# Pairwise bilinear products on one core: three equal store slots in the output ring, two-tile loads of x from GpSimd, and the last load of W without its zeros

## The chip, the cores and the metric

The kernel runs on one core of a Trainium2 chip. The metric is the device time of one execution in microseconds (us). The kernel before was run nine times: the median is 1323.14 us, the lowest 1320.26, the highest 1325.19. A separate profiled execution of it took 1322.69 us.

## The reference, cut to what matters

The input x has 4096 rows, each with 32 fields of 64 numbers (float32). For every pair of fields i < j, 496 in all, there is a 64 x 64 matrix W. The output for a pair is the product of field i with W, multiplied element by element with field j:

```python
i_idx, j_idx = np.triu_indices(32, k=1)
vi = inputs[:, i_idx, :]
vj = inputs[:, j_idx, :]
vdotw = jnp.einsum('bpd,pde->bpe', vi, W)
inter = vdotw * vj
return inter.reshape(B, -1)          # 4096 x (496 * 64)
```

The output is 520 MB, x 33.6 MB, W 8.1 MB. So the kernel writes far more than it reads.

## The kernel before, in words

**Tiles.** The 4096 rows are cut into 32 tiles of 128 rows; a tile puts one row on each partition. The loop over `t` goes through the tiles, and inside it a loop goes through 16 pairs of fields `p`: fields 2p and 2p+1 are first factors together. Field i has 31 - i partners, so its output row segment is (31 - i) units of 64 numbers wide; a tile's output is 496 such units. A unit over 128 partitions is 32,768 bytes.

**Matrix work.** `transpose_x` transposes half a tile on PE (8 blocks of two fields) into PSUM, and ACT copies it to `xT`. Field 2p then lies in the upper 64 partitions and field 2p+1 in the lower 64. For each chunk of up to 512 columns PE multiplies both fields with their columns of W into two banks of the PSUM ring `pring` (8 banks), and VectorE (DVE) multiplies the two banks with the columns of x into the output ring `ring` in SBUF. The transposes of a tile's second half come before pair 3 of the tile; those of the first half come before pair 9 of the tile before it (`SECOND_HALF_AT`, `FIRST_HALF_AT`).

**W.** W is kept in SBUF for the whole kernel: even fields in the upper 64 partitions, odd fields in the lower 64, shifted by one unit, with zeros where the odd rows are shorter. SP loads it in five pieces (`LOADS`), the last for pairs 7 to 15.

**Stores.** `STORES` cuts the 16 pairs of a tile into four groups of 118, 102, 123 and 153 units. When a group is computed, SP issues one DMA of it from the ring to the output, with rows of 26 to 39 KB per partition. The ring has 440 units (`RING = 28160` columns). A group is never split at the ring's end: if it doesn't fit, it begins at the start again,

```python
if at + store_w[s] > RING:
    at = 0
```

and the units behind it stay unused in that round. VectorE may write a part of the ring again only when the store that reads it has landed.

**Loads of x.** Three slots in SBUF hold tiles. Load 0 brings tile 0, loads 1 to 15 bring two tiles each, load 16 brings tile 31. Load k is issued at the start of tile 2k - 2. Tiles in `LIGHT_TILES` (13 even ones) are loaded by GpSimd alone, one tile at a time in rows of 8 KB; the odd tile of the same load is then brought by ACT. The other loads are one ACT DMA each: two with rows of 16 KB for two tiles, two with one tile.

**The DMA engines.** A core has 16 DMA engines. The GpSimd loads are arranged so that engine 4 (`LIGHT`) carries none of them: `load_beside` sends 120 rows, 8 to each of 15 engines that begin with number 5, and the last 8 rows as 4 rows each to two other engines, which `PAIRS_FROM` names in turn. Which engine a GpSimd DMA begins with is kept in `cursor`; `from_engine` moves it on with a tiny DMA, a nudge. So one such load is four DMAs on GpSimd's queue: nudge, 8 rows, nudge, 120 rows. They are kept in program order. The pieces of x in memory are padded so that the access patterns keep this shape; the pads are not read.

Of the kernel before, what the change touches and what calls it, by code (L numbers as in the profile page):

```python
# [9 lines left out]
F32 = mybir.dt.float32  # L10
ALU = mybir.AluOpType

P = 128
BANK = 512
BANKS = 8

STORES = [[0, 1], [2, 3], [4, 5, 6], [7, 8, 9, 10, 11, 12, 13, 14, 15]]

LOADS = [[0], [1], [2, 3], [4, 5, 6], [7, 8, 9, 10, 11, 12, 13, 14, 15]]


FIRST_HALF_AT, SECOND_HALF_AT = 9, 3
RING = 28160

DMA_ENGINES = 16
LIGHT = 4
LIGHT_TILES = [4, 6, 8, 10, 12, 14, 18, 20, 22, 24, 26, 28, 30]
PAIRS_FROM = [6, 8, 10, 12, 14, 0, 1]
HEAD = P // DMA_ENGINES
REST = HEAD // 2  # L30
PAD = 16


def x_slots(NT):


    loads = [[(0, 0)]]
    for t in range(1, NT, 2):
        if t + 1 == NT:
            loads.append([(t, 1)])  # L40
        elif loads[-1][-1] == (t - 1, 2):
            loads.append([(t + 1, 0), (t, 1)])
        else:
            loads.append([(t, 1), (t + 1, 2)])
    return loads


@with_exitstack
def pair_bilinear_kernel(
    ctx: ExitStack,  # L50
    tc: tile.TileContext,
    x: bass.AP,
    w: bass.AP,
    out: bass.AP,
    F: int,
    D: int,
):

    nc = tc.nc
    NT = out.shape[1] * 2 // (F * (F - 1) * D)
    NPR = F // 2

    width = [(F - 1 - i) * D for i in range(F)]
    off = [sum(width[:i]) for i in range(F)]
    cols = sum(width)


    woff = [i % 2 * D + sum(width[i % 2 : i : 2]) for i in range(F)]
    store_w = [sum(width[2 * p] + width[2 * p + 1] for p in g) for g in STORES]

    const = ctx.enter_context(tc.tile_pool(name="const", bufs=1))
    psum = ctx.enter_context(tc.tile_pool(name="ps", bufs=1, space=bass.MemoryType.PSUM))

    ident = const.tile([P, P], F32, tag="ident", name="ident")
    make_identity(nc, ident)

    def runs(tl, a, b, n):  # L100

        ap = tl[:, a : a + n]
        return bass.AP(ap.tensor, ap.offset, [list(ap.ap[0]), [b - a, 2], list(ap.ap[1])])

    xbuf = const.tile([P, 3 * F * D], F32, tag="x", name="x")
    x_loads = x_slots(NT)
    pads = (DMA_ENGINES + 1) * PAD
    tile_sizes = [P * F * D + (pads if t in LIGHT_TILES else 0) for t in range(NT)]
    x_sizes = [sum(tile_sizes[t] for t, s in load) for load in x_loads]
    slot = {t: xbuf[:, ts(s, F * D)] for load in x_loads for t, s in load}  # L110

    nudges = [const.tile([DMA_ENGINES, 16], F32, tag=f"nudge{i}", name=f"nudge{i}") for i in range(2)]
    cursor = 0

    def from_pool(out, in_):

        tc.keep_in_program_order(nc.gpsimd.dma_start(out=out, in_=in_))  # L117

    def from_engine(e):

        nonlocal cursor
        k = (e - cursor) % DMA_ENGINES
        if k:
            nudge = nudges[e == LIGHT + 1]
            from_pool(
                nudge[:k].rearrange("p (h c) -> p h c", h=2)[:, :, :4],
                x[: k * 8].rearrange("(p h c) -> p h c", p=k, h=2),
            )
        cursor = e

    def load_beside(at, xt, lap):

        nonlocal cursor
        most = DMA_ENGINES - 1
        for e, k, rows, p in (
            (PAIRS_FROM[lap % len(PAIRS_FROM)], 2, REST, most * HEAD),
            (LIGHT + 1, most, HEAD, 0),
        ):
            from_engine(e)
            n = rows * F * D  # L140
            blocks = x[at : at + k * (n + PAD)].rearrange("(k c) -> k c", k=k)
            from_pool(xt[p : p + k * rows], blocks[:, :n])
            at += k * (n + PAD)
            cursor = (e + k) % DMA_ENGINES

    def load_x(load):

        at = sum(x_sizes[: x_loads.index(load)])
        parts = [[(t, s)] for t, s in load] if any(t in LIGHT_TILES for t, s in load) else [load]
        for part in parts:  # L150
            t, s = part[0]
            n = len(part) * F * D
            if t in LIGHT_TILES:
                load_beside(at, slot[t], LIGHT_TILES.index(t))
            else:
                nc.scalar.dma_start(
                    out=xbuf[:, s * F * D : s * F * D + n],
                    in_=x[at : at + P * n].rearrange("(p c) -> p c", p=P),
                )
            at += sum(tile_sizes[t] for t, s in part)  # L160

    pring = psum.tile([P, BANKS * BANK], F32, tag="pring", name="pring")
    bank = 0

    def take_banks(n):

        nonlocal bank
        if bank + n > BANKS:
            bank = 0
        got = pring[:, bank * BANK : (bank + n) * BANK]  # L170
        bank = (bank + n) % BANKS
        return got

    xT = const.tile([P, NPR * P], F32, tag="xT", name="xT")

    def transpose_x(xt, g):

        n = 2 * BANK // P
        pt = take_banks(2)
        for c in range(n):  # L180
            nc.tensor.transpose(pt[:, ts(c, P)], xt[:, ts(n * g + c, P)], ident)  # L181
        nc.scalar.copy(xT[:, ts(g, 2 * BANK)], pt)  # L182

    ring = const.tile([P, RING], F32, tag="ring", name="ring")
    at = 0

    load_x(x_loads[0])
    w_sb = const.tile([P, sum(width[0::2])], F32, tag="w", name="w")
    done = 0
    for g in LOADS:  # L190

        upto = woff[2 * g[-1]] + width[2 * g[-1]]
        nc.sync.dma_start(out=w_sb[:, done:upto], in_=w[:, done:upto])
        done = upto

    transpose_x(slot[0], 0)
    for t in range(NT):
        xt = slot[t]
        for load in x_loads:
            if min(load)[0] == t + 1:  # L200
                load_x(load)
        for s, group in enumerate(STORES):
            if at + store_w[s] > RING:
                at = 0
            osb = ring[:, at : at + store_w[s]]
            at += store_w[s]
            o0 = off[2 * group[0]]
            for p in group:
                if p == SECOND_HALF_AT:
                    transpose_x(xt, 1)  # L210
                if p == FIRST_HALF_AT and t + 1 < NT:
                    transpose_x(slot[t + 1], 0)
                first = (width[2 * p] - 1) % BANK + 1
                for c1 in range(first, width[2 * p] + 1, BANK):
                    n = first if c1 == first else BANK
                    c0 = c1 - n
                    odd = width[2 * p + 1] and c1 > D
                    pm = take_banks(2)
                    for h in range(1 + bool(odd)):
                        a = woff[2 * p + h] + c0 - h * D  # L220
                        nc.tensor.matmul(  # L221
                            pm[:, h * BANK : h * BANK + n],
                            xT[h * D : (h + 1) * D, ts(p, P)],
                            w_sb[h * D : (h + 1) * D, a : a + n],
                            start=True,
                            stop=True,
                        )
                    xj = xt[:, (2 * p + 1) * D + c0 : (2 * p + 1) * D + c1]
                    o = [off[2 * p + h] - o0 + c0 - h * D for h in range(2)]
                    if odd and (c0 or c1 < width[2 * p]):  # L230
                        nc.vector.tensor_tensor(  # L231
                            runs(osb, o[0], o[1], n),
                            runs(pm, 0, BANK, n),
                            bass.AP(xj.tensor, xj.offset, [xj.ap[0], [0, 2], xj.ap[1]]),
                            ALU.mult,
                        )
                    else:
                        for h in range(1 + bool(odd)):
                            nc.vector.tensor_tensor(  # L239
                                osb[:, o[h] + h * D : o[h] + n],  # L240
                                pm[:, h * (BANK + D) : h * BANK + n],
                                xj[:, h * D :],
                                ALU.mult,
                            )
            nc.sync.dma_start(
                out=out[:, t * cols + o0 : t * cols + o0 + store_w[s]], in_=osb
            )


# [46 lines left out]
```

## Time and profile before

| What | Value |
|---|---|
| Median of the runs | 1323.14 us (1320.26 to 1325.19) |
| The profiled execution | 1322.69 us, its span 1320.6 us |
| PE (TensorE) busy | 1163.6 us, 88% |
| DVE (VectorE) busy | 1183.4 us, 90%, 1376 instructions |
| ACT (ScalarE), POOL (GpSimd) busy | 66.1 us and 30.2 us |
| DMA | 562.9 MB in 25,404 packets, 426 GB/s over the span |
| Read, written in memory | 41.95 MB, 520.09 MB |

The span is the time from the first to the last instruction on the core; the profiled execution's own time has 2.1 us more around it. The page gives busy time by engine, then 40 equal slices of the span (33 us each) with the busy share in tenths and the rate of the DMA engines in GB/s. Of a DMA queue it tells the packets, the bytes and the share of the 16 engines' span: q1 is SP's queue, q10 ACT's, q0 GpSimd's. Of a group of DMAs it tells how many there are, the size of each and the median time from issue to landing. A line of waits names who waited, for whom, the total in us, how many times, and the longest.

### The profile page before, as it was taken

The numbers are of one execution on the slowest core, as the hardware profiler recorded it, in microseconds if no ns is written. First come the engines' busy times: TensorE is split into PE (matmuls) and PEld (weight loads), VectorE is DVE, ScalarE is ACT, GpSimd is POOL, SyncE is SP. The second block draws the span as 40 slices with busy tenths as digits, with TensorE's granted clock in tenths as the row PEclk, the third lists the DMA queues.
The fourth block names the chain that finished last, engine by engine and source line by source line (L and its number), as shares of the span: only waits on it lengthen the run. The fifth ranks groups of instructions, "written<-read, shape, count | busy, mean of one in ns | idle before, by whom it ended". The sixth has DMA issues, their size and how long they took to land.

```text
span 1320.6 us, 13176 instructions
## 1 busy us (share of the span) xinstructions
PE 1163.6 (88%) x5376; PEld 539.1 (41%) x5376; DVE 1183.4 (90%) x1376; ACT 66.1 (5%) x65; POOL 30.2 (2%) x58
## 2 busy tenths in 40 slices
PE   7998989889898898998899889888988989899993
PEld 3444344343444434444334444334444444343441
DVE  5998999989899898998899899889988989899994
ACT  1000000000000000000000000000000000000000
POOL 0000000000000000000000000000000000000000
PEclk9998999999899998998999989999998999999997
DMA  9999999999999999999999999999999999999998
GB/s 393 431 431 433 427 432 430 426 433 426 427 429 436 419 427 431 431 429 430 426 427 427 430 430 419 433 425 429 429 428 428 416 432 420 437 429 432 427 430 375
DMA packets 25404, 562.90 MB, mean 426 GB/s; under 512 B 4480, under 2 KB 4480, under 8 KB 4736
## 3 DMA queue, kind: packets, MB, share of 16 engines
q1 hardware_dynamic: 19152, 528.49, 93.5%
q10 hardware_dynamic: 2448, 19.92, 3.6%
q0 software_dynamic: 3744, 13.65, 2.5%
q8 instruction: 42, 0.69, 0.2%
q14 instruction: 18, 0.15, 0.0%
HBM read 41.95 MB, written 520.09 MB: 426 GB/s over the span
## 4 chain that ended last, share of the span: by engine, by line
DMA 49%; DVE 34%; PE 8%; issue 8%; DVEq 0%; ACT 0%
DMA out_dram<-ring 49%; DVE ring L231 29%; PE pring L221 7%; DVE ring L239 5%; DMA x<-in_x_dram 1%; DVEq L231 0%; PE pring L181 0%; ACT xT L182 0%; DVEq L292 0%; DVEq L239 0%
## 5 line engine op out<-in xcount | busy, mean ns | idle before, releaser
L221 PE MATMUL pring<-w,xT 64*128 64x512 f32 (+4 forms) x4864 | 1100.4, 562 | 128.5 <-DVE ring L231 108.9
L231 DVE TENSOR_TENSOR ring<-pring,x 128x1024 f32<-128x1024 f32 (+3 forms) x1056 | 1104.8, 1108 | 107.4 <-DMA out_dram<-ring 73.8
L221 PEld LDWEIGHTS pring<-w,xT 64*128 64x128 f32 x4864 | 483.5, 190 | 703.3 <-DVE ring L231 516.4
L182 ACT COPY xT<-pring 128x1024 f32<-128x1024 f32 x64 | 64.8, 1012 | 1209.3 <-PE pring L181 1209.3
L239 DVE TENSOR_TENSOR ring<-pring,x 128x64 f32<-128x64 f32 (+3 forms) x320 | 97.7, 356 | 11.8 <-DMA out_dram<-ring 11.5
L181 PEld LDWEIGHTS pring<-ident,x 128*128 128x128 f32 x512 | 55.7, 142 | 58.1 <-DVE ring L231 49.7
L181 PE MATMUL pring<-ident,x 128*128 128x128 f32 x512 | 70.9, 282 | 8.5 <-DMA x<-in_x_dram 8.4
L117 POOL DMA_DIRECT2D x<-in_x_dram x26 | 15.2, 585 | 1077.9 <-DVE ring L239 1077.6
L117 POOL DMA_DIRECT2D nudge<-in_x_dram x26 | 14.6, 560 | 0.3 <-issue 0.3
L182 ACT ACT_TABLE_LOAD x1 | 1.3, 1283 | 1.7 <-PEq L288 1.7
masks.py:199 POOL TENSOR_SCALAR_AFFINE_SELECT ident<-ident 128x128 f32<-128x128 f32 x1 | 0.3, 288 | 0.1
masks.py:197 POOL MEMSET ident<- 128x128 f32 x1 | 0.2, 204 | 0.3 <-POOLq L288 0.3
L288 POOL MEMSET const-float32-0.0<- 128x1 f32 x1 | 0.1, 98 | 0.2 <-issue 0.2
L288 POOL MEMSET const-bfloat16-1.0<- 128x1 bf16 x1 | 0.1, 101 | 0.0
L288 POOL MEMSET const-uint8-127<- 128x1 uint8 x1 | 0.1, 101 | 0.0
L288 POOL MEMSET const-float32-1.0<- 128x1 f32 x1 | 0.1, 98 | 0.0
## 6 DMA issues: line engine op xcount, KB each, us to landing
out_dram<-ring SPq DMA_DIRECT2D x32, 4896.0 KB, 18.1
out_dram<-ring SPq DMA_DIRECT2D x32, 3936.0 KB, 17.8
out_dram<-ring SPq DMA_DIRECT2D x32, 3776.0 KB, 19.7
out_dram<-ring SPq DMA_DIRECT2D x32, 3264.0 KB, 19.7
x<-in_x_dram ACTq DMA_DIRECT2D x15, 1024.0 KB, 18.6
x<-in_x_dram POOLq DMA_DIRECT2D x13, 960.0 KB, 26.2
x<-in_x_dram ACTq DMA_DIRECT2D x2, 2048.0 KB, 18.2
w<-in_w_dram SPq DMA_DIRECT2D x1, 2592.0 KB, 28.0
```

The lines of the kernel that those rows point to most:

```text
L117: tc.keep_in_program_order(nc.gpsimd.dma_start(out=out, in_=in_))
L181: nc.tensor.transpose(pt[:, ts(c, P)], xt[:, ts(n * g + c, P)], ident)
L182: nc.scalar.copy(xT[:, ts(g, 2 * BANK)], pt)
L221: nc.tensor.matmul(pm[:, h * BANK : h * BANK + n], xT[h * D : (h + 1) * D, ts(p, P)], w_sb[h * D : (h + 1) * D, a : a + n], start=True, st ...
L231: nc.vector.tensor_tensor(runs(osb, o[0], o[1], n), runs(pm, 0, BANK, n), bass.AP(xj.tensor, xj.offset, [xj.ap[0], [0, 2], xj.ap[1]]), ALU ...
L239: nc.vector.tensor_tensor(osb[:, o[h] + h * D : o[h] + n], pm[:, h * (BANK + D) : h * BANK + n], xj[:, h * D :], ALU.mult,)
L288: nc = bacc.Bacc("TRN2", target_bir_lowering=False, num_devices=1)
```

## The change

**Stores.** `STORES` goes. The output of all 32 tiles is taken as one stream of 15,872 units, which runs through the ring to its very end and on from its start. `ends` cuts the stream: the first round of the ring into 118, 102, 110 and 110 units, each later round into 147, 147 and 146, the last piece is the 32 units that remain. A new function `made` counts what of each piece is still missing and issues a piece's store when it is complete. A new function `multiply` does VectorE's product and cuts a chunk where it passes the ring's end; where the two fields' halves are no longer in ascending order in the ring, it makes two instructions of one.

**Loads of x.** `LIGHT_TILES` becomes `LIGHT_LOADS`: six whole loads (3, 5, 8, 10, 13 and 15) are brought by GpSimd, both tiles at once in rows of 16 KB; all others are one ACT DMA each. The two engines for the last 8 rows are (5, 6), (7, 8), (9, 10), (11, 12), (13, 14) and (15, 0) in turn. A nudge of one step gets a form of its own, which these six loads don't use.

**W.** The last of the five loads stops at column 15,424, where the odd fields end; a sixth DMA brings the remaining 960 columns for the upper 64 partitions alone.

```diff
-STORES = [[0, 1], [2, 3], [4, 5, 6], [7, 8, 9, 10, 11, 12, 13, 14, 15]]
+ROUND = [147, 147, 146]
+FIRST_ROUND = [118, 102, 110, 110]
...
-RING = 28160
+RING_UNITS = sum(ROUND)
...
-LIGHT_TILES = [4, 6, 8, 10, 12, 14, 18, 20, 22, 24, 26, 28, 30]
-PAIRS_FROM = [6, 8, 10, 12, 14, 0, 1]
+LIGHT_LOADS = [3, 5, 8, 10, 13, 15]
+PAIRS_FROM = [5, 7, 9, 11, 13, 15, 1, 2, 0, 14, 12, 10, 8, 6]
...
-    store_w = [sum(width[2 * p] + width[2 * p + 1] for p in g) for g in STORES]
+    ring_w = RING_UNITS * D
+    ends = [0]
+    while ends[-1] < NT * cols:
+        for units in ROUND if ends[-1] else FIRST_ROUND:
+            ends.append(min(ends[-1] + units * D, NT * cols))
+            if ends[-1] == NT * cols:
+                break
+    missing = [b - a for a, b in zip(ends, ends[1:])]
+    stored = 0
...
-        at = sum(x_sizes[: x_loads.index(load)])
-        parts = [[(t, s)] for t, s in load] if any(t in LIGHT_TILES for t, s in load) else [load]
-        for part in parts:
...
+        i = x_loads.index(load)
+        at = sum(x_sizes[:i])
+        n = len(load) * F * D
+        s = load[0][1]
+        xt = xbuf[:, s * F * D : s * F * D + n]
+        if i in LIGHT_LOADS:
+            load_beside(at, xt, n, LIGHT_LOADS.index(i))
+        else:
+            nc.scalar.dma_start(out=xt, in_=x[at : at + P * n].rearrange("(p c) -> p c", p=P))
...
+    def multiply(tos, pm, xj, n):
+
+        at = [to % ring_w for to in tos]
+        cuts = {ring_w - a for a in at if a < ring_w < a + n}
+        for i, j in zip([0, *sorted(cuts)], [*sorted(cuts), n]):
+            a = [(to + i) % ring_w for to in tos]
+            if len(tos) == 2 and a[0] < a[1]:
+                xs = xj[:, i:j]
+                nc.vector.tensor_tensor(
+                    runs(ring, a[0], a[1], j - i),
...
+                continue
+            for h, b in enumerate(a):
+                nc.vector.tensor_tensor(
+                    ring[:, b : b + j - i],
...
+    def made(a, b):
+
+        nonlocal stored
+        for i in range(stored, len(missing)):
+            missing[i] -= max(0, min(b, ends[i + 1]) - max(a, ends[i]))
+        while stored < len(missing) and not missing[stored]:
+            a, b = ends[stored : stored + 2]
+            nc.sync.dma_start(
+                out=out[:, a:b], in_=ring[:, a % ring_w : a % ring_w + b - a]
+            )
+            stored += 1
...
-        nc.sync.dma_start(out=w_sb[:, done:upto], in_=w[:, done:upto])
+        odd = woff[F - 1] + width[F - 1]
+        both = min(upto, odd)
+        nc.sync.dma_start(out=w_sb[:, done:both], in_=w[:, done:both])
+        if both < upto:
+            nc.sync.dma_start(out=w_sb[:D, both:upto], in_=w[:D, both:upto])
...
-                        nc.vector.tensor_tensor(
-                            runs(osb, o[0], o[1], n),
...
-            nc.sync.dma_start(
-                out=out[:, t * cols + o0 : t * cols + o0 + store_w[s]], in_=osb
-            )
+                if odd and (c0 or c1 < width[2 * p]):
+                    multiply(o, pm, xj, n)
+                else:
                     for h in range(1 + bool(odd)):
...
+                        multiply([o[h] + h * D], pm[:, h * (BANK + D) :], xj[:, h * D :], n - h * D)
+                for h in range(1 + bool(odd)):
+                    a = o[h] + (0 if c0 else h * D)
+                    made(a, o[h] + n)
```

## The prediction

> **What bounds the kernel now.** I began with the page: its shares, its DMA rates by slice, its queues and its DMA issues.
>
> ```profile
> span 1320.6 us, 13176 instructions
> ...
> PE 1163.6 (88%) x5376; PEld 539.1 (41%) x5376; DVE 1183.4 (90%) x1376; ACT 66.1 (5%) x65; POOL 30.2 (2%) x58
> ...
> DMA  9999999999999999999999999999999999999998
> GB/s 393 431 431 433 427 432 430 426 433 426 427 429 436 419 427 431 431 429 430 426 427 427 430 430 419 433 425 429 429 428 428 416 432 420 437 429 432 427 430 375
> DMA packets 25404, 562.90 MB, mean 426 GB/s; under 512 B 4480, under 2 KB 4480, under 8 KB 4736
> ...
> q1 hardware_dynamic: 19152, 528.49, 93.5%
> q10 hardware_dynamic: 2448, 19.92, 3.6%
> q0 software_dynamic: 3744, 13.65, 2.5%
> ...
> out_dram<-ring SPq DMA_DIRECT2D x32, 4896.0 KB, 18.1
> out_dram<-ring SPq DMA_DIRECT2D x32, 3936.0 KB, 17.8
> out_dram<-ring SPq DMA_DIRECT2D x32, 3776.0 KB, 19.7
> out_dram<-ring SPq DMA_DIRECT2D x32, 3264.0 KB, 19.7
> x<-in_x_dram ACTq DMA_DIRECT2D x15, 1024.0 KB, 18.6
> x<-in_x_dram POOLq DMA_DIRECT2D x13, 960.0 KB, 26.2
> ```
>
> The DMA engines are busy in every slice and move 562.9 MB, of which 520.1 MB are output. At the 431 GB/s of an ordinary slice that is 1306 us: the DMA engines are the bound, and only fewer bytes, fewer packets or fewer gaps on them can shorten the kernel. Then the waits: VectorE works 1183 us and has spare time, which it spends on room in the ring.
>
> ```profile
> DVE ring L231 <- DMA out_dram<-ring: 73.8, 43, 6.2
> DVE ring L239 <- DMA out_dram<-ring: 11.5, 6, 2.1
> ```
>
> That is 85 us of slack on VectorE. Last, stretches of time, whose final two columns are DMA share and GB/s.
>
> ```profile
> 28.00:30.00 2.00, 2.00 (x12) 0.97 (x10) 2.00 (x3) 0.00 (x0) 0.00 (x0) 1.00 0.79 243
> 30.00:40.00 10.00, 9.82 (x44) 3.50 (x42) 9.71 (x10) 0.00 (x0) 0.00 (x0) 1.00 1.01 432
> 40.00:1300.00 1260.00, 1133.06 (x5250) 525.52 (x5248) 1155.66 (x1344) 62.75 (x62) 28.81 (x51) 0.98 1.00 429
> 1314.00:1321.00 7.00, 0.00 (x0) 0.00 (x0) 0.00 (x0) 0.00 (x0) 0.00 (x0) 0.50 0.23 101
> ```
>
> Undisturbed the engines move 432 GB/s, over the long middle 429. The middle's difference is (432-429)/432 x 1260 = 8.7 us. Part of it is in dips: slices 14, 25, 32 and 34 have 416 to 420. I looked into slice 32:
>
> ```profile
> 1024.00:1028.00 4.00, 4.00 (x23) 2.83 (x22) 4.00 (x8) 0.00 (x0) 2.24 (x4) 1.00 0.98 412
> 1028.00:1034.00 6.00, 5.46 (x24) 1.67 (x21) 5.71 (x7) 0.00 (x0) 0.00 (x0) 1.00 0.98 417
> 1034.00:1040.00 6.00, 5.79 (x30) 2.83 (x30) 6.00 (x8) 1.01 (x1) 0.00 (x0) 1.00 0.98 392
> ```
>
> At 1025.2 SP issues the tile's fourth store, and GpSimd its load. In the trace's DMA records the store before ends between 1024.7 and 1029.3 us, engine by engine, 1026.5 on average: the first engines were out of work when the next store came. The same holds at 458, 661, 783 and 1107. So before each fourth store the backlog is nearly gone. The page agrees: 4896 KB take 11.6 us at 431 GB/s and land after 18.1, 6.5 us later; for 3264 KB that is 19.7 - 7.8 = 11.9. The fourth store is the longest to fill (153 of 496 units: 11.4 us) and follows one of 9.4 us. Summing what the records leave unused around those handovers gives 3.2 us per engine.
>
> **What the Trainium skill says.** *DMA: Bandwidth & Descriptors*, "Queues, rings and completion order": an engine goes round-robin between its queues by packet. The trace agrees: 64 KB from GpSimd take 13.2 us to land, since each small packet waits for one row of a store (1.0 to 1.45 us). "Why a DMA increments its semaphore by 16": a GpSimd transfer posts an increment on all 16 engines and takes k engines from a cursor. The trace shows more still, two 4-byte packets per engine and transfer. "Why small descriptors are slow": some 3 cycles per packet. The records agree: 8192 B took 309 ns, 16384 B 611, 39168 B 1448, so 302 ns per 8 KB (27.2 B/ns) and 7 or 8 ns fixed, of which 3 overlap the packet before: 4 net, 6 for a semaphore packet of 9 ns.
>
> **The change, part by part** (per DMA engine).
>
> *Stores*: 128 become 110 (4, then 35 rounds of 3, then one of 32 units). 18 x 128 rows fewer: 144 per engine x 4 ns = 0.58 us. *Loads of x*: 3840 rows become 2176 (two ACT loads of 8 KB rows, fifteen of 16 KB): 104 x 4 ns = 0.42 us. *Small packets*: stores and W 17 fewer per engine, ACT 6, GpSimd 7 of 13 loads x 160 / 16 = 70; 93 x 6 ns = 0.56 us. *W*: 64 rows x 3840 B not read, 245,760 B / 435 GB/s = 0.56 us; the extra SP issue costs 0.45 us behind five others, hidden since SP's first store is at 23.3. The slow stretch at 28 to 30 us, the last rows of W, I leave as it is. Sum 2.1 us. Without the overlap (8 and 9 ns) it would be 3.4; I take 2.1.
>
> *The ring.* Before, three stores fill 343 to 394 of the 440 units and the rest is skipped. Now a slot of 147 units fills in 147 x 1183.4/15872 = 11.0 us and drains in 147 x 32,768 B / 431 GB/s = 11.2, with its share of loads (33.55 MB over 110 stores) 11.9. When one slot has landed, VectorE starts on it while one full slot drains and the next is just issued, so it has some 11.9 us in hand. A pair that straddles a boundary needs the next slot before its own is complete: up to 61 units x 75 ns = 4.6 us less, so 7 us or more remain where the fourth store has 0 to 4 now. No handover should starve. What it is worth is bounded by zero (the engine that ends last never starved) and the 3.2 us of the records. I take 2.3, since nine or more of sixteen engines were level after such a handover (at 662 us), so most engines, the later last one included, had lost time in some.
>
> *VectorE*: stepping through the loops, chunks cut at the ring's end make 1376 instructions 1483. The forms 1024 and 64 long (1217, 216 ns) give 149 ns fixed: at most 107 x 149 ns = 16 us, paid from the 85 us of slack. Without that cover it would be 16 us.
>
> *The six GpSimd loads.* Before, such a load brought the even tile, released a tile early; now it brings both, released as ACT's are, at the tile's start. On GpSimd's queue four DMAs go out in 2.2 us; nothing waits there behind them. The nine two-tile ACT loads are issued where ACT's loads are now, with the xT copies behind them as before, and landed in 18.2 us where there were such. Before, the 960 KB landed 26.2 us after issue, 1.7 us behind the first. Now store rows of 37,632 B instead of 31,744 on average: 0.22 us more for each of about 19 packets (4.1 us), and 8 to 12 rows longer by 0.30 us (2.4 to 3.6): 34.4 to 35.6 us after release. PE's transposes of the next tile come 29.6 to 33 us after release (the timeline; 253.8 to 285.6 for one), so PE waits some 4 us, VectorE about 3 (it has three or four chunks in banks): 18 us in six loads, hidden by VectorE's remaining 69 us of slack and, each time, by the 7 us of backlog. Behind PE stand the pairs from 9 on, behind them VectorE and the next store.
>
> *The engine that is spared* (4): before 13 x 64 KB, now 6 x 128 KB. It moves x for 16 x 607 + 120 x 305 ns = 46.3 us before and 16 x 305 + 72 x 607 = 48.6 after, so it gains nothing: +2.3 - 1.7 (2.1 less the 0.42 for x) = +0.6 us. In the records it falls behind the mean by about 2% of the time while engines compute, and after each such load is early again. I judge it not last, since it starved most, being early at the handovers.
>
> Sum: -2.1 - 2.3 = -4.4 us. The profiled execution took 1322.7 us (span 1320.6 and 2.1 around it), so 1318.3; the median of the runs is 0.4 above: 1323.1 - 4.4 = **1318.7**.
>
> **Rivals.** (1) *As summed*, 0.55, own range 1316.8 to 1320.4. For it: the dips; against it: only the engine that ends last counts. (2) *The last engine never starved*, 0.18: only the 2.1 us remain, 1321.0. For it: the last four of sixteen engines end 1 to 2.5 us after the mean of 1316.6, and those are not early at handovers. (3) *The spared engine ends last*, 0.08: +0.6, so 1323.7; for it: in the records it ended 2.15 us after the mean. (4) *More*, 0.09: the dips and lags go with smaller packets too, twice 2.3 and a level end, 1316. (5) *The late loads starve the DMA engines*, 0.10, slower: if a two-tile load lands past 34 + 7 = 41 us after release, the stores run out, and each us beyond costs one, six times. At 43 us: +12 - 4.4, 1331. For it: 26.2 us is a median, one load took 27.5; against it: once the stores run out, nothing delays the load, and my 35.6 is 5 us below.
>
> **How the numbers follow.** A measurement here tells about 0.2%, 2.6 us, from no change. Faster: nearly all of (1), (4), and a little of (2): 0.64. Same: (2), (3), the edge of (1): 0.26. Slower: (5), 0.10. The range leaves out most of (5) and the far end of (4): 1314.5 to 1323.3.
>
> **What would show it.** Packets: near 20,000, 562.6 MB. No slice in the middle under 424 GB/s, the middle at 430 or more. Stores of 4704 KB landing 20 to 24 us after issue. VectorE 1195 to 1200 us busy, waits on the ring's stores about 50 to 70 us. GpSimd's x loads landing 31 to 36 us after issue, with PE waiting for x up to six times by a few us. It would be wrong if the tail at the end grows (engines without gaps drift apart), if slices stay at 416, or if waits on x run to 10 us.

## The result, and the profile after

The changed kernel takes 1318.62 us (median of 15 runs, 1317.15 to 1320.40) against 1322.58 us for the kernel before in the same comparison: a ratio of 0.9970, with a 95% interval of 0.9962 to 0.9977. That is 4.0 us less, between 3.0 and 5.0. The forecast was 4.4 us less, 1318.7 us. Its profiled execution took 1318.62 us, with a span of 1316.8: 3.8 us less than the span before.

The page of the changed kernel, the lines that answer to those shown of before:

```profile
span 1316.8 us, 13125 instructions
...
PE 1171.5 (89%) x5376; PEld 554.9 (42%) x5376; DVE 1188.8 (90%) x1483; ACT 66.1 (5%) x65; POOL 14.4 (1%) x30
...
GB/s 390 432 430 433 432 427 436 429 435 432 428 432 429 431 430 435 429 429 430 430 432 434 428 432 425 432 433 426 436 425 426 428 414 433 431 425 432 427 432 362
DMA packets 20012, 562.64 MB, mean 427 GB/s; under 512 B 2992, under 2 KB 2992, under 8 KB 3312
...
q1 hardware_dynamic: 16640, 528.24, 93.4%
q10 hardware_dynamic: 1584, 20.97, 3.8%
q0 software_dynamic: 1728, 12.59, 2.3%
...
out_dram<-ring SPq DMA_DIRECT2D x70, 4704.0 KB, 20.9
out_dram<-ring SPq DMA_DIRECT2D x35, 4672.0 KB, 21.5
x<-in_x_dram ACTq DMA_DIRECT2D x9, 2048.0 KB, 20.9
x<-in_x_dram POOLq DMA_DIRECT2D x6, 1920.0 KB, 31.4
```

The bound is the same, the DMA engines. There are 5392 packets and 0.26 MB fewer. The four dips in the slices are gone (slices 14, 25, 32 and 34 have 431, 425, 428 and 433 now), and slice 33 has a new one, 414. A second profile of the same kernel has 419, 421, 423 and 419 in slices 6, 23, 31 and 33: only the one in slice 33 is in both. A store of 4704 KB needs 11.2 us at 431 GB/s and lands after 20.9, 9.7 us later; for the fourth store before this difference was 6.5. It holds more than the work queued ahead of the store: also the loads' rows in between, and the lag of the slowest engine.

The list of waits of the changed kernel, in us, times and the longest; the last line is PE waiting for x ahead of its transposes:

```profile
DVE ring L203 <- DMA out_dram<-ring: 45.4, 23, 6.0
...
DVE ring L211 <- DMA out_dram<-ring: 20.2, 11, 5.0
...
PE pring L190 <- DMA x<-in_x_dram: 15.8, 3, 8.5
```

VectorE waits for room 65.6 us instead of 85.3. Of PE's three waits for x the longest, 8.5 us, is the first load of the kernel, which was there before; the two others are the late two-tile loads, 7.3 us together. Stretches of time, the last two columns being DMA share and GB/s:

```profile
40.00:1300.00 1260.00, 1141.80 (x5250) 541.64 (x5246) 1162.89 (x1457) 62.74 (x62) 12.98 (x23) 0.97 1.00 430
...
1310.00:1317.00 7.00, 0.00 (x0) 0.00 (x0) 0.00 (x0) 0.00 (x0) 0.00 (x0) 0.50 0.27 116
```

The middle goes at 430 GB/s instead of 429. The tail is about as long as before: in the DMA records the sixteen engines end at 1312.5 us on average and the last one at 1315.5, where it was 1316.6 and 1319.1.

### The profile page after: what moved, and what is told of

The parts are those of the page before. It is cut to its first block, busy times and chain, and to the rows that moved or that the text cites. A ratio compares the mean times of both kernels' runs of the same rounds, so it can differ in the third digit from the quotient of the medians.

```text
span 1316.8 us, 13125 instructions
## 1 busy us (share of the span) xinstructions
PE 1171.5 (89%) x5376; PEld 554.9 (42%) x5376; DVE 1188.8 (90%) x1483; ACT 66.1 (5%) x65; POOL 14.4 (1%) x30
## 2 busy tenths in 40 slices
DMA packets 20012, 562.64 MB, mean 427 GB/s; under 512 B 2992, under 2 KB 2992, under 8 KB 3312
## 4 chain that ended last, share of the span: by engine, by line
DMA 35%; DVE 32%; issue 6%; PE 4%; DVEq 0%; POOL 0%
DMA out_dram<-ring 33%; DVE ring L203 26%; DVE ring L211 6%; PE pring L262 4%; DMA x<-in_x_dram 3%; PE pring L190 1%; DVEq L203 0%; POOL x L127 0%; POOL nudge L127 0%; DVEq L316 0%; DVEq L211 0%
## 5 line engine op out<-in xcount | busy, mean ns | idle before, releaser
L203 DVE TENSOR_TENSOR ring<-pring,x 128x1024 f32<-128x1024 f32 (+4 forms) x1012 | 1043.5, 1093 | 77.8 <-DMA out_dram<-ring 45.4
L262 PEld LDWEIGHTS pring<-w,xT 64*128 64x128 f32 x4864 | 497.2, 190 | 665.4 <-DVE ring L203 453.7
L211 DVE TENSOR_TENSOR ring<-pring,x 128x64 f32<-128x64 f32 (+7 forms) x471 | 168.9, 413 | 27.6 <-DMA out_dram<-ring 20.2
L127 POOL DMA_DIRECT2D x<-in_x_dram x12 | 7.0, 585 | 1122.9 <-DVE ring L211 1122.9
L127 POOL DMA_DIRECT2D nudge<-in_x_dram x12 | 6.8, 565 | 0.3 <-issue 0.3
## 6 DMA issues: line engine op xcount, KB each, us to landing
out_dram<-ring SPq DMA_DIRECT2D x70, 4704.0 KB, 20.9
x<-in_x_dram ACTq DMA_DIRECT2D x9, 2048.0 KB, 20.9
x<-in_x_dram POOLq DMA_DIRECT2D x6, 1920.0 KB, 31.4
```

What stands on the lines that cost most here:

```text
L203: nc.vector.tensor_tensor(runs(ring, a[0], a[1], j - i), runs(pm, i, BANK + i, j - i), bass.AP(xs.tensor, xs.offset, [xs.ap[0], [0, 2], xs ...
L211: nc.vector.tensor_tensor(ring[:, b : b + j - i], pm[:, h * BANK + i : h * BANK + j], xj[:, i:j], ALU.mult,)
L262: nc.tensor.matmul(pm[:, h * BANK : h * BANK + n], xT[h * D : (h + 1) * D, ts(p, P)], w_sb[h * D : (h + 1) * D, a : a + n], start=True, st ...
```

## The experiments

"Handover" is below the moment at which an engine has finished a store and takes up the next. From the DMA records I counted at how many handovers the first of the sixteen engines had less than 1.3 us of work left when SP issued the next store. An issued DMA needs about 1 us to its first packet: the kernel's first one was issued at 0.74 us and its packets began at 1.75. Such a handover is called starved below. Before, there were 16 of 127; after, 9 of 109.

### The ring alone

```diff
 (kernel before)
-STORES = [[0, 1], [2, 3], [4, 5, 6], [7, 8, 9, 10, 11, 12, 13, 14, 15]]
-RING = 28160
+ROUND = [147, 147, 146]
+FIRST_ROUND = [118, 102, 110, 110]
 ... multiply(), made() and the loop of the changed kernel; loads as before
```

> The kernel before with the new ring alone (three slots, 110 stores); loads of x and W as before. Theory (handovers): the packets of 18 fewer stores are worth 18 x (8 x 4 + 6) ns = 0.7 us, the backlog that no longer runs out 2.3 us: 3.0 us faster than before, about 1319.6. Rival (only packets and bytes count, the last engine never starved): 0.7 us faster, 1321.9. Rival (the gain lies in the loads from GpSimd): also 0.7 us.

Measured: median 1319.70 us (22 runs) beside 1323.32 for before; the ratio is 0.9986 (0.9975 to 0.9997); two of its runs lay at 1327. By the medians the gain is 3.6 us, by the ratio 1.9. The starved handovers fall to 6 of 109. The interval, 0.4 to 3.3 us, holds the 3.0 of the handover theory and the 0.7 of the rivals; only the median, and the idle time in its profile (the table in the section on the prediction), speak for the first.

### The loads of x and W alone

```diff
 (kernel before, ring and stores unchanged)
-LIGHT_TILES = [4, 6, 8, 10, 12, 14, 18, 20, 22, 24, 26, 28, 30]
+LIGHT_LOADS = [3, 5, 8, 10, 13, 15]
 ... load_x(), load_beside(), x on the host and the two last loads of W as in the changed kernel
```

> The kernel before with the new loads alone: six two-tile loads from GpSimd and W without its zeros; the ring and its four stores a tile as before. Theory (handovers): 104 fewer rows x 4 ns, 76 fewer small packets x 6 ns and 0.56 us of W are 1.4 us, the handovers starve as before: 1.4 us faster, about 1321.2. Rival (small GpSimd packets cost much more than their 6 ns, and the gain lies there): 3.3 us faster, 1319.3. Rival (late two-tile loads starve the engines where the backlog is small): slower than before.

Measured: median 1327.53 us, ratio 1.0035 (1.0020 to 1.0050): slower by 4.6 us, where I had put it 1.4 us faster. Its waits and its middle:

```profile
DVE ring L235 <- DMA out_dram<-ring: 82.5, 33, 6.4
...
PE pring L181 <- DMA x<-in_x_dram: 19.0, 5, 8.6
```

```profile
40.00:1300.00 1260.00, 1123.11 (x5208) 525.37 (x5208) 1146.14 (x1335) 62.74 (x62) 12.99 (x23) 0.97 1.00 425
```

The middle falls from 429 to 425 GB/s. The starved handovers rise from 16 to 24, and at the worst one the engines had been out of work for 0.4 us on average when the store came. Summed over the DMA records between 40 and 1300 us, an engine stands without a packet for 8.0 us, where it was 2.7 before. So the loads do not pay on their own; they lose, and the larger part of it is starvation.

### The changed kernel beside its halves

> The changed kernel itself, beside its two halves on one chip. Theory: the two halves add up, 4.4 us faster than before. Rival: they overlap (both only take gaps away that the other would take too) and this one is no faster than the better half.

Measured on the same chip as the two halves: median 1318.85 us, ratio 0.9971 (0.9963 to 0.9979), 3.8 us faster than before. The halves do not add up: 3.6 us gained (by medians) and 4.2 lost would give a kernel slower than before. On the new ring the same loads are not slower any more; by medians they gain 0.9 us, within what the intervals leave open. So with the old four stores the two-tile loads lose, and on the new ring no loss is to be seen.

### The spared engine

```diff
 (changed kernel)
-LIGHT_LOADS = [3, 5, 8, 10, 13, 15]
+LIGHT_LOADS = []
```

> The changed kernel with no load from GpSimd: all loads of x are two-tile DMAs from ACT, so engine 4 is no longer spared. Theory (engine 4 falls behind by some 2% while the core computes): it carries 6 x 128 KB more, 29 us, and was 2 to 3 us ahead of the mean at the end, so it ends last by far: 20 to 26 us slower than the changed kernel, about 1338 to 1344. Rival (its lag is small or belongs to the profile alone): within 2 us of the changed kernel.

Measured: median 1338.60 us, 19.8 us slower than the changed kernel beside it (1318.85): within the times I gave, and just below the 20 to 26 us. Stretches at its end, DMA share and GB/s last:

```profile
1320.00:1326.00 6.00, 0.00 (x0) 0.00 (x0) 0.00 (x0) 0.00 (x0) 0.00 (x0) 0.50 0.97 419
1326.00:1330.00 4.00, 0.00 (x0) 0.00 (x0) 0.00 (x0) 0.00 (x0) 0.00 (x0) 0.50 0.62 263
1330.00:1337.00 7.00, 0.00 (x0) 0.00 (x0) 0.00 (x0) 0.00 (x0) 0.00 (x0) 0.50 0.05 20
```

From 1330 us on 20 GB/s are moved, less than one engine's 27: a single engine is left with work. It lags long before: from 300 to 1300 us, the engine that ends a store last is 5 to 11 us behind the mean of the sixteen at each handover, where it is at most 4.8 in the changed kernel (5.4 in its second profile). The store's slot comes free only when this engine is done, and the other fifteen run dry: 31 of 109 handovers are starved, and an engine stands without a packet for 8.0 us on average. So one engine is slower, and the time without a profile shows the cost too. The records do not name engines; that it is number 4 is what the code's `LIGHT` says. The lag is not the whole of the 19.8 us: the 16 KB rows of ACT's loads take 666 ns on average here, against 622 in the changed kernel. Whether the lag causes that too is open.

### The fourth store cut in two

```diff
 (kernel before, nothing else changed)
-STORES = [[0, 1], [2, 3], [4, 5, 6], [7, 8, 9, 10, 11, 12, 13, 14, 15]]
+STORES = [[0, 1], [2, 3], [4, 5, 6], [7, 8, 9], [10, 11, 12, 13, 14, 15]]
```

> The kernel before with its fourth store (153 units) cut into two of 87 and 66; nothing else. Theory (handovers starve): the long fill ahead of the fourth store goes, 2.3 us and perhaps all 3.2 us of unused time, for 32 more stores at 38 ns = 1.2 us: 1 to 2 us faster than before. Rival (only packets count): 1.2 us slower. Rival (more pieces hold the ring longer and make other handovers starve): slower by more than 2 us.

Measured: median 1318.86 us, ratio 0.9973 (0.9965 to 0.9981): 3.6 us faster than before, with 32 stores and 4610 packets more. This is the clearest evidence that it matters where the stores are cut: the edit adds DMA work and changes nothing but the cut, and with it the length of the rows (22,272 and 16,896 B instead of 39,168). No handover of 159 is starved, and no slice of its middle lies below 425:

```profile
GB/s 394 426 432 434 429 430 426 431 434 427 433 428 428 433 430 428 433 426 433 432 429 428 434 425 430 432 427 433 426 429 436 427 429 430 429 433 433 430 430 351
...
out_dram<-ring SPq DMA_DIRECT2D x32, 2784.0 KB, 21.4
out_dram<-ring SPq DMA_DIRECT2D x32, 2112.0 KB, 21.1
```

The two halves of the old fourth store now land 21.4 and 21.1 us after issue, though they need only 6.6 and 5.0 us themselves at 431 GB/s. With 1.2 us of packets by my price on top of the measured 3.6, the cut is worth about 4.8 us, an estimate: more than the 2.3 I took and the 3.2 I had called the upper bound. Not all of it is time without work; the section on the prediction splits it.

### Six slots, and four

```diff
 (changed kernel; first the one, then the other)
-ROUND = [147, 147, 146]
+ROUND = [74, 73, 74, 73, 73, 73]
+ROUND = [110, 110, 110, 110]
```

> The changed kernel with the ring in six slots of 73 or 74 units: 214 stores instead of 110, rows half as long. Theory (a store costs its 8 x 4 + 6 ns on each engine): 104 x 38 ns = 4.0 us slower than the changed kernel. Rival (what counted in the change was only room in the ring, and finer pieces give more of it): equal or faster. Rival (packets cost their full 8 and 9 ns): 7.6 us slower.

Measured: median 1326.76 us, about 8 us slower than the changed kernel (1318.6 and 1318.9 elsewhere), with no starved handover of 214. That is the figure of the rival with full packets, but the trace tells otherwise. The records give 104 more stores 3.8 us, as I had priced them, and the rest falls into the GpSimd loads: in their stretches some 3.5 us more are left unused than in the changed kernel (the second profile of that one makes it some 3). One such stretch, first here and then in the changed kernel:

```profile
576.00:588.00 12.00, 8.68 (x33) 3.97 (x34) 7.91 (x9) 1.01 (x1) 0.00 (x0) 0.86 1.01 381
```

```profile
576.00:588.00 12.00, 11.18 (x50) 5.16 (x48) 9.95 (x13) 1.01 (x1) 0.00 (x0) 1.00 1.02 429
```

> The changed kernel with the ring in four slots of 110 units: 145 stores. Theory: 35 x 38 ns = 1.3 us more for packets; three slots already leave a backlog at nearly every handover, so no more than 1 us comes back: 0.3 to 1.3 us slower than the changed kernel. Rival (engine 4, early by 4.9 us after each two-tile load, still runs out of stores with three slots): 1 to 2 us faster.

Measured: median 1319.51 us, ratio 0.9979 (0.9972 to 0.9985). No handover of 144 is starved, and the price of 35 more stores is not quite won back: 0.7 to 0.9 us slower than the changed kernel by medians, as expected. In time, three slots are enough.

### Less ring

```diff
 (kernel before)
-RING = 28160
+RING = 24576
 (changed kernel)
-ROUND = [147, 147, 146]
-FIRST_ROUND = [118, 102, 110, 110]
+ROUND = [128, 128, 128]
+FIRST_ROUND = [118, 102, 82, 82]
```

> The kernel before with a ring of 384 units instead of 440; stores as before, so rounds of 343, 373 and 276 units. Theory (room in the ring sets the backlog): stepping through two tiles with 75 ns per unit to fill and 76 ns to drain, two or three handovers starve by 1 to 2 us each, 4 us in two tiles, 64 us in all: 1360 to 1400. Rival (room does not matter, VectorE has 85 us to spare): 1323.

Measured, one run: 1438.92 us, 116 us slower than before and well past the range I gave. 51 of 127 handovers are starved; its slices:

```profile
GB/s 397 429 434 339 421 378 373 434 341 420 391 375 432 330 429 387 382 431 334 422 388 381 431 341 432 358 388 432 337 420 367 389 425 328 420 395 395 387 389 386
```

> The changed kernel with a ring of 384 units in three slots of 128 (125 stores), the size at which the kernel before lost 116 us. Theory (with a ring that is used to its end and even pieces the backlog shrinks only in proportion, by an eighth): 0.6 to 1.1 us for 15 more stores and up to 1.5 us of gaps, 1319.5 to 1321.5. Rival (it is the ring's size that counts): many tens of us slower.

Measured: median 1320.84 us, ratio 0.9987 (0.9979 to 0.9994): still faster than the kernel before with its full ring. The same eighth of the ring costs the old cut 116 us and the three even slots about 2. So room in the ring counts with the old cut, and the three slots have some to spare. They differ from it in two ways, pieces of equal size and no unused end of the ring; which of the two does it was not separated. By my count 18 of 124 handovers are starved here, two more than in the kernel before, and yet it is faster: the count of first engines alone does not give the time.

### Four stores, more even

```diff
 (kernel before, nothing else changed)
-STORES = [[0, 1], [2, 3], [4, 5, 6], [7, 8, 9, 10, 11, 12, 13, 14, 15]]
+STORES = [[0, 1], [2, 3, 4], [5, 6, 7], [8, 9, 10, 11, 12, 13, 14, 15]]
```

> The kernel before with its four stores made more even: 118, 147, 111 and 120 units instead of 118, 102, 123 and 153; still 128 stores. Theory (the long fill ahead of the fourth store empties the backlog): the longest fill is 11.0 us against a drain of 9.0 before it, and only once a tile, as before 11.4 against 9.4, but two stores follow it that drain as fast as they fill: part of the 3.2 us of gaps goes, 1 to 3 us faster than before. Rival (the waste at the ring's end alone sets the backlog; rounds of 376, 385 and 349 units are no better than 343 to 394): no change.

Measured: median 1317.08 us, ratio 0.9957 (0.9945 to 0.9970): 5.7 us faster than before, with the same 128 stores, packets and loads, and well above the 1 to 3 us I expected. It is the fastest kernel of this study by the median; its interval and that of the changed kernel (0.9962 to 0.9977) still overlap a little. The starved handovers fall from 16 to 7, and all stores wait about alike:

```profile
out_dram<-ring SPq DMA_DIRECT2D x32, 4704.0 KB, 19.3
out_dram<-ring SPq DMA_DIRECT2D x32, 3840.0 KB, 19.2
out_dram<-ring SPq DMA_DIRECT2D x32, 3776.0 KB, 19.8
out_dram<-ring SPq DMA_DIRECT2D x32, 3552.0 KB, 19.8
```

### The loads on a kernel with backlog, and W alone

```diff
 (kernel before with the fourth store cut in two)
 first:  loads of x and W as in the changed kernel
 second: loads of W alone as in the changed kernel
```

> The kernel with the new loads of x and W (which alone were slower than before) and the fourth store cut in two. Theory (those loads lost time because late x and engines that are 5 us early met a small backlog): with a backlog they are free and their fewer packets count, 1.4 to 2 us faster than the kernel with the cut store alone: about 1317. Rival (two-tile loads from GpSimd cost DMA time by themselves): 4 us slower than that kernel, 1323.

Measured: median 1324.01 us, ratio 1.0010 (1.0002 to 1.0018): 5 us slower than with the cut store alone. My theory was that the loads lose time only through late x and a small backlog. It falls here: there is a backlog (4 starved handovers of 159, and 1.2 us without a packet, as with the cut store alone), PE waits for no x but the first, and the two-tile loads still cost 5 us. Three stretches of it, the middle one with the two-tile load that was issued at 980.3:

```profile
975.00:988.00 13.00, 12.12 (x60) 6.38 (x58) 12.72 (x19) 0.00 (x0) 2.25 (x4) 1.00 0.99 424
988.00:1002.00 14.00, 13.25 (x62) 5.20 (x58) 13.29 (x14) 1.01 (x1) 0.00 (x0) 1.00 1.01 380
1002.00:1020.00 18.00, 16.07 (x76) 8.28 (x76) 16.05 (x24) 1.01 (x1) 0.00 (x0) 0.91 1.01 433
```

While its rows come in, the engines are fully busy (share 1.01) and move only 380 GB/s; the kernel with W alone (below), which has no such load there, moves 440 from 988 to 1002 us. In the records a 16 KB row of these loads takes 679 ns on average, against 624 in the changed kernel and 612 for ACT's rows of the same size in this very kernel. Each engine has 48 of them: at 67 ns more that is 3.2 us of the 5, and the stores' rows lose 1.9 us more than with the cut store alone. The size of the stores' rows does not explain it: GpSimd's rows take 680 ns with six slots (rows of 18 KB), 628 with four (27.5 KB) and 657 with three slots of 128 units (32 KB). One thing goes with it. In this kernel GpSimd's rows take 611 ns while fewer than three rows of loads are in flight, and 782 with nine to eleven; ACT's take 614 with nine to eleven. ACT's rows are not immune (see the spared engine). What slows them I have not found out.

> The kernel before with the fourth store cut in two and W without its zeros, loads of x as before. Theory: 0.56 us less than with the cut store alone, about 1318.3. Rival (W's load lies ahead of the first store and its bytes do not reach the end): no different from the cut store alone.

Measured: median 1318.40 us, ratio 0.9966 (0.9954 to 0.9979), against 0.9973 for the cut store alone. The difference, 0.5 us by medians of two comparisons, has the predicted size and is smaller than the intervals. It shows nothing either way.

## Why the prediction was right, and where it was not

**The bound and the sum.** The DMA engines stayed the bound, and the time came out as summed, 1318.6 for 1318.7. Part of that is luck: the kernel before ran at 1322.58 in this comparison and not at 1323.14, and the difference is 4.0 for 4.4. The packets (20,012 for near 20,000), the bytes and the waits of VectorE on the ring (65.6 us for 50 to 70) came out as said.

**The ring.** That the cut of the stores costs time was right: cutting the fourth store gained 3.6 us and four even stores 5.7, and packets alone would have given a loss of 1.2 and no change. What was too small is the term: I took 2.3 us of a supposed limit of 3.2. The records show why, if what an engine loses is added up between 40 and 1300 us: the time without a packet, and the time that rows of stores take beyond the commonest for their size (1448 ns for 39,168 B, for one). All in us; the change in time is by the ratio, the last two columns are from one profile each.

| Kernel | Change in time | Starved handovers | Without a packet | Rows too slow |
|---|---|---|---|---|
| before | | 16 of 127 | 2.7 | 9.0 |
| ring alone | -1.9 | 6 of 109 | 0.8 | 6.5 |
| changed kernel | -4.0 | 9 of 109 | 1.5 | 6.3 |
| fourth store cut | -3.6 | 0 of 159 | 1.1 | 4.9 |
| four even stores | -5.7 | 7 of 127 | 1.0 | 5.9 |
| three slots, 384 units | -1.7 | 18 of 124 | 1.2 | 6.3 |
| loads of x and W alone | +4.6 | 24 of 127 | 8.0 | 13.5 |

The four even stores have the same packets as before, so the split can be read there: the engines stand idle 1.7 us less, and rows lose 3.1 us less. Together that is 4.8, and the spans of the two profiles differ by 4.9. Of the slow rows before, 1.5 us lie at the starved handovers, where engines that ran dry begin again at the same moment: at 418.24 us five rows begin within 0.06 us and take 1760 ns or more instead of 1448. With four even stores that is 0.1. Another 5.4 us before, and 3.8 with even stores, lie where rows of the loads of x are in flight; why even stores make these fewer is not shown. So the starved handovers account for some 3 us of this gain, if all the idle time is put down to them, and not for all of it; I had left slow rows out. A second profile of the changed kernel has 7.6 instead of 6.3 in the last column, so differences of about 1 us in it mean nothing.

**"No handover should starve"** failed in part. I gave every handover 7 to 12 us of backlog. The records of the changed kernel show 2.2 us at the smallest and 6.4 on average over engines, hardly more than the 6.2 before, and 9 starved first engines. The step left out how far the engines stand apart: after the GpSimd load near 1146 us one engine is 5.2 us ahead of the mean, and it was first to run out.

**The loads of x** were the step that failed. I put 0.42 us of rows and some 0.45 us of small packets to their credit; with W's saving included they lost 4.6 us alone, and 5 us on a kernel with backlog. My fifth rival had them late and starving the engines. Alone they do that (24 starved handovers, 5.3 us more without a packet); in the changed kernel they land as forecast (31.4 us after issue; PE waits for two-tile loads twice, in the second profile four times). The loss without starvation in the kernel with the cut store shows a second cause: the rows themselves become slow. By the medians the right sum was two errors against each other, and so in part luck: the ring brought 3.6 us where I had put 3.0 with its packets, the loads and W 0.9 where I had put 1.4. The intervals are too wide to hold these shares apart.

**The packets.** The price of 4 and 6 ns was shown by the six slots only through the records (3.8 us of work for 104 stores); the time went up by twice that for another reason.

**VectorE** worked 1188.8 us, not 1195 to 1200: 107 more instructions cost 5.4 us, 50 ns each rather than 149. It was hidden, as said.

**The spared engine** does need its sparing: 20 us without it. The rival in which it ends last and costs 0.6 us did not come about in the time; as the records name no engines, that another one ended last is not shown.

**Slices.** No slice was to lie under 424; slice 33, at 414, does, and in the second profile slices 6, 23 and 31 as well. In slice 33 an ACT load is issued at 1056.5 us; five rows of a store that begin at 1058.2 take 2142 to 2378 ns instead of 1382, and the load's own rows then 684 on average instead of 611 (701 in the second profile). Why is open.

## What to carry to other kernels

When the DMA engines are the bound, look at the moments between their transfers: a transfer that takes longer to compute (11.4 us for the fourth store) than the one ahead of it takes to drain (9.4) empties the queue, and the average busy share hides it. Do not look at empty queues alone: rows that take longer than usual cost more here. Pieces of more even size gained at least as much (5.7 us for one line) as a new ring and new loads together (4.0 us). Test the parts of a change apart: one of these halves was a loss that the other covered.

## What the runs showed of the hardware that was not expected

- One of the sixteen DMA engines is slower: without its sparing the kernel took 19.8 us longer, and from 300 to 1300 us one engine was 5 to 11 us behind the mean of the sixteen at each handover.
- 16 KB rows that GpSimd loads took 679 ns on average in the kernel with the cut store, ACT's 612 in the same kernel: 380 GB/s in such a stretch at full share. With nine to eleven rows of loads in flight it was 782 and 614.
- Rows of stores that begin together after the engines ran dry took 1760 ns instead of 1448.
- An eighth less ring cost 116 us with unsplit, uneven pieces and about 2 us with three even ones that use the ring to its end.
